# Where the second group's tokens are queued on VectorE in a sorted attention

## The chip, the cores and the metric

The kernel runs on one core of one Trainium2 chip. The metric is the device time of one execution in microseconds; the time of a version is the median over its runs. A profile is one further execution, recorded instruction by instruction. In what follows PE is TensorE (matmuls; PEld its weight loads), DVE is VectorE, ACT is ScalarE, POOL is GpSimd, SP is SyncE. L1454 means line 1454 of the kernel before the change.

## What is computed

Two layers, each an attention-like block and a feed-forward block, on x of 16 x 256 tokens with 512 features, all in float32. Cut to what matters here:

```python
x = x + conv_attention(layernorm(x), k, skip, ctx, ctx)     # layer 0
x = x + routed_ffn(layernorm(x), ...)                       # 8 experts, top 2, and a shared one
x = x + latent_attention(layernorm(x), ctx, seg_id, ...)    # layer 1: the stage that is changed
x = x + ffn(layernorm(x), proj1, proj2, ...)

# latent_attention: 16 heads; a query with segment id s sees the keys s-8 .. s only
q_c = q @ W_dq
scores = (q_nope . k_nope + rope(q_c @ W_qr) . rope(k_rope)) / sqrt(192)
attn = softmax(where((k <= s) & (k >= s - 8), scores, -1e30))
out = (attn @ v) @ W_o
```

The input of the latent attention is the output of the routed layer: per token, its row of x plus two expert rows, each times a gate, then a layernorm.

## The kernel before

The 4096 tokens are sorted by batch and segment id, so that 32 neighbours share a window of 32 keys. The stage `attention_sorted` goes through them in 32 tiles of 128 tokens, T = 0 to 31. Four tiles are a group g with t = T % 4. The queries are made per group: group 0 partly ahead of the loop and partly in its first two passes, group g + 1 while group g is attended. This case is about group 1, tiles 4 to 7, prepared in the passes T = 0 to 3.

What one pass does, in the order in which the program traces it:

- `scores(T)`: small matmuls of queries and window keys into a PSUM tile of its own tag (L1563, L1569). It needs `qn`, `qr` and the window's `kn` and `krz`.
- `weigh(T)`, on DVE: a 32x32-block transpose into `e` (L1579), the mask (L1581), the row maximum (L1585), its subtraction (L1586).
- `values(T-1)`: matmuls of the last pass's attention weights and the gathered keys (L1609), copied out by ACT (L1615).
- `weights(e)`: exp on ACT (L1590), then on DVE the row sums (L1592), reciprocals (L1594), the product (L1595) and a transpose back into `at` (L1597).
- `window(T+1)`: the next window's keys are transposed on PE (L1535, L1540) and copied by ACT (L1537, L1542); its mask is made on DVE (L1548 to L1551).
- `heads`: in T = 0 and 1 the second half of group 0's queries, in every t = 3 the next group's. PE L1501 to L1512; ACT copies (L1517, L1525); the rope on DVE (L1519) and POOL (L1520, L1521). In t = 3, `latents` (L1473, L1484), which `heads` needs, is traced ahead of `values(T-1)`; it reads all four token tiles of the next group.
- `project(T-2)`: 16 matmuls (L1625, 32 in the records), an add on DVE (L1630), a store from POOL's queue (L1631).

`tokens(st, t)` prepares one tile of the next group: two fused multiply-adds of gathered expert rows onto the token row (DVE, L1454, twice), a layernorm by `bn_stats` and `bn_aggr` (DVE, L66 and L68), the inverse root on POOL (L70, L71), the scaling (DVE, L72); then the rope rows' transpose `prr` (PE, L1462) and the row's own transpose `pt` (PE, L99), copied by ACT (L1463, L100).

Rows come by indirect DMAs that POOL issues (all at L1919): `xt` (token rows), `rr` (rope rows), `gw` (the window's keys, four per pass, by `fetch_keys(T + 2)`) and the expert rows, shown as `w<-ygd,slot_s`. The expert rows have four buffers in rotation, two to a tile, so a tile's gathers must wait until the tile two before it has been added. Group 1's tiles are traced at these places: tile 4 at T = 2 after `weigh`; tile 5 at the end of T = 2; tiles 6 and 7 at T = 3 after `weigh` and ahead of `latents`. The gathers of tile 4 are traced at T = 0 and those of tile 5 at T = 1, behind the heads of that pass.

No order is written out for this stage. A program that runs when the kernel is built decides the order of the instructions on each engine: it walks through them with a model of the engines, and gives each engine what is ready, earlier traced work first. `with tc.issue_after(ins):` restricts it: what the block traces on the engine of `ins` is queued behind `ins`. This sets an order only; nothing waits for `ins` to end beyond what an engine does in working through its queue. Instructions in the block on other engines are not held by it.

A tile from a pool takes one of the buffers of its tag. `prr`, `pt`, `pq`, `pqr`, `pqn`, `pkw`, `prw`, `pu` and `po` all have the tag "m" with seven PSUM buffers.

Of the kernel before, what the change touches and what calls it, by code (L numbers as in the profile page):

```python
# [13 lines left out]
ALU = mybir.AluOpType  # L14
# [4 lines left out]
P = 128  # L19
# [15 lines left out]
CQ, WIN = 8, 32  # L35
# [7 lines left out]
class Kernel:  # L43
# [1343 lines left out]
    def attention_sorted(self, fetched, ygd, x3s, end_of_queries):  # L1387
        nc, tc = self.nc, self.tc
        wdq, m0, m1, wqr0, wqr1, nw = self.wdq, self.m0, self.m1, self.wqr0, self.wqr1, self.nw
        fetch, fetch_keys, xs, rrs, gws, _ = fetched  # L1390
        T4 = 4
# [4 lines left out]
        with ExitStack() as ctx:  # L1396
# [41 lines left out]
            def fetch_routed(st, t):  # L1438
                T = st["g"] * T4 + t
                st["y"].append([])  # L1440
                for k in range(2):
                    yt = g_yt[rows_fetched[0] % 4]
                    rows_fetched[0] += 1
                    self.fetch_rows(yt, ygd, self.slot_s[:, k, T : T + 1], NT * P)
                    st["y"][t].append(yt)

            def tokens(st, t):

                T = st["g"] * T4 + t
                if t == 0:  # L1450
                    st["xT"], st["rope"] = g_xT, g_rope
                xt, yts, rr = xs[T], st["y"][t], rrs.pop(T)
                for k in range(2):
                    nc.vector.scalar_tensor_tensor(  # L1454
                        xt, yts[k], self.routes[:, T, 2 + k : 3 + k], xt, ALU.mult, ALU.add
                    )
                xh = tp.tile([P, D], F32, tag="xh", name="xh")
                self.layernorm(xh, xt, small)
                toks = slice(t * P, (t + 1) * P)
                pt = ps_m.tile([P, 2, P], F32, tag="m", name="prr")  # L1460
                for i in range(2):
                    nc.tensor.transpose(pt[:, i, :], rr[:, i, :], self.ident)  # L1462
                nc.scalar.copy(st["rope"][:, :, toks], pt)  # L1463
                self.transposed(st["xT"][:, :, toks], xh, ps_m, "m")
# [60 lines left out]
                        nc.scalar.copy(qn[:, cs, c0 : c0 + CQ], by_chunk(pqn[k][i]))  # L1525
                return turned

            wins, last_at = {}, [None]

            def window(T):  # L1530
                gw = gws.pop(T)
# [21 lines left out]
            def scores(st, T):  # L1553

                w, t = wins[T], T % T4
                s = ps_s.tile([P, 4 * P], F32, tag="s", name="ps")
                for a in range(4):
                    for piece in range(3):
                        for j in range(4):
                            c = t * 16 + a * 4 + j  # L1560
                            r = slice(j * WIN, (j + 1) * WIN)
                            if piece == 0:
                                nc.tensor.matmul(  # L1563
                                    s[r, a * P : (a + 1) * P], w["kn"][:, a, r], qn[:, c, :],
                                    start=(a == 0), stop=False, skip_group_check=True,
                                )
                            else:
                                c0 = a * P + (piece - 1) * (P // 2)
                                nc.tensor.matmul(  # L1569
                                    s[r, c0 : c0 + P // 2], krz[piece - 1][:, a, r], qr[:, c, :],  # L1570
                                    start=False, stop=True, skip_group_check=True,
                                )
                return s

            def weigh(T, s):

                e = ap_.tile([P, 16, WIN], F32, tag="e", name="e")
                flat = e.rearrange("p x k -> p (x k)")
                nc.vector.transpose(flat, s)  # L1579
                e4 = e.rearrange("p (a h) k -> p a h k", h=4)  # L1580
                nc.vector.tensor_tensor(  # L1581
                    e4, e4, wins[T]["mask"].unsqueeze(2).to_broadcast([P, 4, 4, WIN]), ALU.add
                )
                mx = small.tile([P, 16], F32, tag="mx", name="mx")
                nc.vector.tensor_reduce(mx, e, AX.X, ALU.max)  # L1585
                nc.vector.tensor_tensor(e, e, mx.unsqueeze(2).to_broadcast([P, 16, WIN]), ALU.subtract)  # L1586
                return e

            def weights(e):
# [31 lines left out]
            def project(st, T, ut):  # L1621
                po = ps_m.tile([P, D], F32, tag="m", name="po")
                for n in range(HEADS):
                    i, hp = n // HP, n % HP
                    nc.tensor.matmul(  # L1625
                        po, ut[:, n].rearrange("p a j q -> p (a j q)"), nw[:, 2 * hp + i, :],
                        start=(n == 0), stop=(n == HEADS - 1),
                    )
                xt = xs.pop(T)
                nc.vector.tensor_tensor(xt, xt, po, ALU.add)  # L1630
                nc.gpsimd.dma_start(x3s[T // T4][T % T4 * P : (T % T4 + 1) * P, :], xt)  # L1631
# [6 lines left out]
            TH = T4 // 2  # L1638
# [15 lines left out]
            for T in range(NT_ + 2):  # L1654
                g, t = T // T4, T % T4
                if T < NT_:
                    if 3 <= T + 2 < NT_:
                        fetch_keys(T + 2)
                    s = scores(state[g], T)
                    e = weigh(T, s)  # L1660
                    nxt = state.setdefault(g + 1, new(g + 1)) if g + 1 < NG else None

                    if nxt is not None:
                        for k in () if g == 0 else ((0,), (2,), (), ())[t]:
                            fetch((g + 1) * T4 + k)
                            fetch_routed(nxt, k)
                    if nxt is not None and g == 0 and t == 2:
                        with tc.issue_after(turned):
                            tokens(nxt, 0)
                        fetch(T4 + 2)  # L1670
                        fetch_routed(nxt, 2)
                    if nxt is not None and g == 0 and t == 3:
                        for k in range(TH, T4):
                            tokens(nxt, k)
                    if nxt is not None and t == 3:
                        latents(nxt)
                if 1 <= T <= NT_:
                    uts[T - 1] = values(T - 1, ats.pop(T - 1))
                if T < NT_:
                    ats[T] = weights(e)  # L1680
                    if T + 1 < NT_:
                        window(T + 1)
                    if T < 2:
                        for two in range(T * HP // 4, (T + 1) * HP // 4):
                            turned = heads(state[0], two, parts[1])

                        with tc.issue_after(turned):
                            fetch(T4 + T)
                            fetch_routed(nxt, T)
                    if nxt is not None and t == 3:  # L1690
                        for two in range(HP // 2):
                            heads(nxt, two)
                if T >= 2:
                    project(state[(T - 2) // T4], T - 2, uts.pop(T - 2))
                if T >= NT_:

                    if T == NT_:
                        end_of_queries()
                    which = T - NT_
                    xT = self.e_w2[:, which * DC * N : (which + 1) * DC * N].rearrange("p (c x) -> p c x", c=DC)  # L1700
                    for k in range(T4):
                        xt = ap_.tile([P, N], F32, tag="sw", name="xt", bufs=3)
                        nc.sync.dma_start(xt, x3s[which][k * P : (k + 1) * P, :])
                        xh = tp.tile([P, D], F32, tag="xh", name="xh")
                        self.layernorm(xh, xt, small)
                        self.transposed(xT[:, :, k * P : (k + 1) * P], xh, ps_m, "m")
                if T < NT_ and nxt is not None:
                    if g == 0:
                        if t == 2:
                            tokens(nxt, 1)  # L1710
                            fetch(T4 + 3)
                            fetch_routed(nxt, 3)
                    else:
                        if t == 0:
                            fetch((g + 1) * T4 + 1)
                            fetch_routed(nxt, 1)
                        for k in ((0,), (1,), (2, 3), ())[t]:
                            tokens(nxt, k)
                        if t == 1:
                            fetch((g + 1) * T4 + 3)  # L1720
                            fetch_routed(nxt, 3)
# [365 lines left out]
```

## Time and profile before

| | us |
|---|---|
| median of 3 runs | 3074.01 (3070.93 to 3077.48) |
| the profiled execution | 3075.3 |
| its span, first to last instruction | 3073.5 |
| PE busy in it | 3000.4 |
| DVE busy | 1434.6 |
| POOL busy | 921.1 |
| ACT busy | 661.8 |
| the sorted attention, passes T = 0 to 3, until the scores of T = 4 begin | about 1283 to 1452 |

A row of the timeline gives start and duration in us, engine, line, operation, output and input names, shapes and count; in square brackets the idle time of the engine ahead of it and what ended that. The busy time of PE is pipelined work and no measure of its peak; what counts here is where it is idle, and the granted clock: TensorE runs at full (1.00) or half (0.50) clock in these rows.

### The profile page before, as it was taken

How to read it: one execution, taken by the hardware profiler on the slowest of the kernel's cores; microseconds unless marked ns; L12 is line 12 of the kernel's file. 1: busy time of each engine (PE TensorE's matmuls, PEld its weight loads, DVE VectorE, ACT ScalarE, POOL GpSimd, SP SyncE). 2: the span in 40 equal slices, each digit the busy share in tenths (PEclk: the TensorE clock that was granted, in tenths of full speed). 3: DMA queues.
4: the chain of work that ended last, by engine and by line, in shares of the span. 5: the costliest groups of instructions: out<-in, count | busy, mean ns of one | idle time of the engine just before them, and what ended most of it. 6: DMA issues, size and time to landing. Idle time of an engine off the chain costs nothing.

```text
span 3073.5 us, 34728 instructions
## 1 busy us (share of the span) xinstructions
PE 3000.4 (98%) x12825; PEld 1529.7 (50%) x12825; DVE 1434.6 (47%) x2652; ACT 661.8 (22%) x1250; POOL 921.1 (30%) x1270
## 2 busy tenths in 40 slices
PE   7999999999999999889999999999999999999998
PEld 4444444444455666554554554454444444444443
DVE  6877777776764444443433433443333222222222
ACT  1111111111111111243333323324121111111110
POOL 2233233232223300165545555534110300301201
PEclk9999999999999999989999999999999999999999
DMA  4232221211115653311211221212120100100100
GB/s 118 70 107 88 59 63 57 67 60 60 56 41 184 208 164 129 111 52 45 86 53 53 74 66 46 69 53 70 58 103 28 55 14 14 55 10 11 45 0 29
DMA packets 119218, 209.87 MB, mean 68 GB/s; under 512 B 27592, under 2 KB 47976, under 8 KB 118400
## 3 DMA queue, kind: packets, MB, share of 16 engines
q1 hardware_dynamic: 90752, 125.63, 13.6%
q0 software_dynamic: 28288, 81.92, 8.3%
q8 instruction: 105, 1.72, 0.2%
q14 instruction: 73, 0.60, 0.1%
HBM read 140.12 MB, written 67.37 MB: 68 GB/s over the span
## 4 chain that ended last, share of the span: by engine, by line
PE 87%; DVE 6%; issue 4%; POOL 2%; DMA 1%; ACT 0%; SPq 0%; POOLq 0%; DVEq 0%; ACTq 0%
PE y L292 15%; PE po L1879 14%; PE ph L1821 13%; PE po L1625 11%; PE phg L895 4%; PE pog L914 4%; PE pqn L1504 4%; PE pout L503 3%; PE ph L490 3%; PE pqr L1501 2%; PE pqn L1512 2%; PE pt L99 2%; PE pqr L1508 1%; DVE pr L297 1%; PE ptg L884 1%
## 5 line engine op out<-in xcount | busy, mean ns | idle before, releaser
L292 PE MATMUL y<-kv,ut 128*128 128x512 f32 x1280 | 562.4, 594 | 0.6 <-DVE pr L297 0.6
L1625 PE MATMUL po<-nw,w 128*128 128x512 f32 x1024 | 445.7, 593 | 0.0
L1879 PE MATMUL po<-p,ht 128*128 128x512 f32 x1024 | 445.1, 592 | 0.0
L292 PEld LDWEIGHTS y<-kv,ut 128*128 128x128 f32 x1280 | 242.1, 191 | 295.6 <-issue 286.1
L1625 PEld LDWEIGHTS po<-nw,w 128*128 128x128 f32 x1024 | 192.0, 190 | 235.1 <-issue 229.6
L1879 PEld LDWEIGHTS po<-p,ht 128*128 128x128 f32 x1024 | 192.7, 190 | 233.4 <-issue 232.2
L1821 PE MATMUL ph<-w,w 128*128 128x512 f32 x640 | 281.2, 592 | 0.0
L297 DVE TENSOR_TENSOR pr<-y,cT 128x512 f32<-128x512 f32 x256 | 174.7, 682 | 143.3 <-PE y L292 143.3
L1883 DVE TENSOR_TENSOR res<-res,po 128x512 f32<-128x512 f32 x128 | 87.8, 686 | 315.4 <-PE po L1879 315.4
L1821 PEld LDWEIGHTS ph<-w,w 128*128 128x128 f32 x640 | 121.5, 190 | 152.6 <-issue 152.6
L304 DVE TENSOR_REDUCE oT<-pr 128x64 f32<-128x512 f32 x256 | 175.7, 686 | 8.8
L274 DVE TENSOR_TENSOR kv<-pvt,cT 128x512 f32<-128x512 f32 x256 | 174.1, 681 | 0.0
L1919 POOL DMA_INDIRECT gw<-kvd,keys_of x128 | 133.3, 1041 | 49.9 <-issue 37.8
L267 POOL TENSOR_TENSOR xt<-xt,sk 128x512 f32<-128x512 f32 x32 | 40.7, 1271 | 338.8 <-DVE sk L266 298.4
L1519 DVE TENSOR_TENSOR w<-pqr,w 128x512 f32<-128x512 f32 (+1 forms) x72 | 45.4, 632 | 203.0 <-ACT sw L1517 189.5
L895 PE MATMUL phg<-w,xTg 128*128 x568 | 134.6, 380 | 0.2
L914 PE MATMUL pog<-w,hT 128*128 x284 | 133.6, 593 | 0.0
L1504 PE MATMUL pqn<-w,m 128*128 128x512 f32 (+1 forms) x288 | 117.0, 548 | 7.2 <-ACT kn L1537 7.1
L490 PE MATMUL ph<-xT,w_s 128*128 128x512 f32 x256 | 118.4, 607 | 0.0
L1821 PE MATMUL ph<-xT,w 128*128 128x512 f32 x256 | 116.4, 592 | 0.0
L1835 ACT ACTIVATE ht<-ht,p1b 128x512 f32<-128x512 f32 x96 | 69.3, 722 | 212.7 <-DVE ht L1840 212.7
L503 PE MATMUL pout<-w_s,ht 128*128 128x512 f32 x256 | 113.6, 593 | 0.0
(291 smaller groups left out, 3773.9 us busy)
## 6 DMA issues: line engine op xcount, KB each, us to landing
xg<-xgd SPq DMA_DIRECT2D x71, 256.0 KB, 2.7
ygd<-y SPq DMA_DIRECT2D x71, 256.0 KB, 2.0
xt<-in_x_dram SPq DMA_DIRECT2D x32, 256.0 KB, 3.5
ct<-in_ctx_dram SPq DMA_DIRECT2D x32, 256.0 KB, 3.4
ut<-in_kt_dram SPq DMA_DIRECT2D x32, 256.0 KB, 2.6
w<-in_w_dram SPq DMA_DIRECT2D x8, 1024.0 KB, 5.5
x1d<-xt SPq DMA_DIRECT2D x32, 256.0 KB, 2.9
x3s<-xt POOLq DMA_DIRECT2D x32, 256.0 KB, 2.9
```

The costliest lines, as they stand in the source:

```text
L274: nc.vector.tensor_tensor(c["kv"][half][:, mc, :].rearrange("p (b j i) -> p b j i", i=NH, j=NH), c["vt"][:, mc, cols].rearrange("p (b i) - ...
L292: c["conv"] = nc.tensor.matmul(y, ut[:, (lc - mc) * P : (lc - mc + 1) * P], kv[:, mc, :], start=(mc == 0), stop=(mc == lc),).ins
L297: nc.vector.tensor_tensor(pr, y.rearrange("p (b j i) -> p b j i", i=NH, j=NH), cT[:, lc, cols].rearrange("p (b i) -> p b i", i=NH) .unsque ...
L304: nc.vector.tensor_reduce(c["oT"][:, lc, cols].rearrange("p (b j) -> p b j", j=NH), pr, AX.X, ALU.add)
L490: nc.tensor.matmul(ph, w["sw1"][:, c, f * P : (f + 1) * P], xT[:, c, :], start=(c == 0), stop=(c == DC - 1),)
L503: nc.tensor.matmul(po, st["ht"][f][:, tok], w["sw2"][:, f, :], start=(f == 0), stop=(f == NC_ - 1))
L895: nc.tensor.matmul(ph, xT[:, c, :], w1[:, c, bass.ds(e * EH, EH)], start=(c == 0), stop=(c == DC - 1))
L914: nc.tensor.matmul(po, hT[:, q, :], w2[:, bass.ds(e * (EH * D // P) + q * D, D)], start=(q == 0), stop=(q == EH // P - 1),)
L1504: nc.tensor.matmul(pqn[k][i], m0[:, 2 * hp + i, :], q0, start=True, stop=False)
L1625: nc.tensor.matmul(po, ut[:, n].rearrange("p a j q -> p (a j q)"), nw[:, 2 * hp + i, :], start=(n == 0), stop=(n == HEADS - 1),)
L1821: nc.tensor.matmul(ph, w[:, c, :], x[:, c, :], start=(start and c == 0), stop=(c == half - 1), skip_group_check=True,)
L1879: nc.tensor.matmul(po, ht[f, i // T4][:, toks], w2[:, f, :], start=(f == fs[0]), stop=(f == fs[-1]))
```

## The change

`weigh` keeps its last DVE instruction, the subtraction of the maximum, as `last_e[0]`. The tokens of group 1 are then traced inside `issue_after` blocks: tile 4 behind the subtraction of T = 2 (it keeps its older block, which concerns POOL), tile 5 behind the last transpose of T = 2 (`last_at[0]`, L1597), tiles 6 and 7 behind the subtraction of T = 3. This queues their L1454, L66, L68 and L72 behind those instructions on DVE. Nothing is added to the computation or taken from it, and the places where things are traced stay the same. Groups 2 to 7 are traced by other lines and are not touched.

```diff
-            wins, last_at = {}, [None]
+            wins, last_at, last_e = {}, [None], [None]
...
-                nc.vector.tensor_tensor(e, e, mx.unsqueeze(2).to_broadcast([P, 16, WIN]), ALU.subtract)
+                last_e[0] = nc.vector.tensor_tensor(
+                    e, e, mx.unsqueeze(2).to_broadcast([P, 16, WIN]), ALU.subtract
+                ).ins
                 return e
...
                     if nxt is not None and g == 0 and t == 2:
-                        with tc.issue_after(turned):
+                        with tc.issue_after(turned), tc.issue_after(last_e[0]):
                             tokens(nxt, 0)
                         fetch(T4 + 2)
                         fetch_routed(nxt, 2)
                     if nxt is not None and g == 0 and t == 3:
-                        for k in range(TH, T4):
-                            tokens(nxt, k)
+                        with tc.issue_after(last_e[0]):
+                            for k in range(TH, T4):
+                                tokens(nxt, k)
...
                         if t == 2:
-                            tokens(nxt, 1)
+                            with tc.issue_after(last_at[0]):
+                                tokens(nxt, 1)
                             fetch(T4 + 3)
                             fetch_routed(nxt, 3)
```

## The prediction

> **What bounds the kernel now.** I read the page first. TensorE is busy nearly everywhere, so a change pays or costs only what it does to TensorE's gaps:
>
> ```profile
> PE 3000.4 (98%) x12825; PEld 1529.7 (50%) x12825; DVE 1434.6 (47%) x2652; ACT 661.8 (22%) x1250; POOL 921.1 (30%) x1270
> ```
>
> The changed lines trace work of steps T = 2 and 3 of the sorted attention. I looked for those by stretches of time (length, busy time of PE, PEld, DVE, ACT and POOL, then the granted clock, DMA share, GB/s):
>
> ```profile
> 1333.00:1349.00 16.00, 15.99 (x215) 12.71 (x206) 8.39 (x17) 11.06 (x25) 8.27 (x11) 1.00 0.04 11
> 1349.00:1380.00 31.00, 17.95 (x183) 13.49 (x182) 14.92 (x31) 10.19 (x26) 24.41 (x27) 0.72 0.38 105
> 1380.00:1452.00 72.00, 71.22 (x330) 32.34 (x328) 21.70 (x44) 28.86 (x54) 40.93 (x42) 1.00 0.17 49
> ```
>
> One stretch is bad: 31 us with 13.05 us of idle TensorE and a mean clock of 0.72; it is the step from T = 1 to T = 2. Behind it TensorE is full. The timeline says why:
>
> ```profile
> 1345.00 0.72 DVE L1579 STREAM_TRANSPOSE e<-ps 128x512 f32<-128x512 f32 x1 [0.75 <-PE ps L1569]
> 1351.20 0.75 DVE L1454 SCALAR_TENSOR_TENSOR xt<-w,routes,xt 128x512 f32<-128x512 f32 x1 [5.48 <-DMA w<-ygd,slot_s]
> 1351.87 0.69 DVE L1581 TENSOR_TENSOR e<-e,mask 128x512 f32<-128x512 f32 x1
> ...
> 1354.50 0.68 DVE L1586 TENSOR_TENSOR e<-e,mx 128x512 f32<-128x512 f32 x1
> 1355.74 0.57 ACT L1537 COPY kn<-pkw 128x512 f32<-128x512 f32 x1
> 1356.36 1.22 PE L1504 MATMUL pqn<-w,m 128*128 128x256 f32 x2 [7.14 <-ACT kn L1537]
> ```
>
> The softmax of T = 1 is cut after its first instruction by the tokens of the second group, though they are traced at T = 2: VectorE sits 5.48 us before L1454 until gathered rows land, L1581 queues behind that, then exp and the kn copy on ScalarE, and TensorE loses 7.14 us. Call the second group's tiles k0 to k3. The gather at 1352.22 waits for an L1454, so it fetches into k0's buffers: it is k2's, and k2 too is joined in this softmax (1355.76, 1357.32). k1 and k3 follow at 1375.31 and 1381.64.
>
> **Part 1, the stall that goes: a gain.** Every VectorE instruction of k0 and k2 that stands between L1579 and L1597 of T = 1 (four L1454, one L66, one L68) leaves it. An uncut softmax runs from the start of L1579 to the end of L1586 in 2.97 us (T = 4: 1454.27 to 1457.24), so T = 1's ends at 1347.97. ScalarE is at its pu copies until 1348.11, exp takes 0.63, kn is copied by 1349.2, where TensorE stops today. The 7.14 us go, and so does the half clock after them: TensorE worked 5.9 us (1356.36 to 1362.3) at 0.5, half of it lost, 3.0. heads of T = 1 end near 1356 instead of 1365.7.
>
> What is late next is POOL, in order. Today 1349.99 to 1363.22 goes to k2's two gathers, the four of the key window, and two of the third group; then the rope adds (L1520, L1521) take 5.74 until 1368.96, and scores of T = 2 waits for them. k2's gathers (they overwrite k0's buffers) and the third group's (k2's buffers) now have to follow the moved L1454, so they leave. The key gathers stay: 1350.29 + 5.55 + 5.74 = 1361.6. The rope part of scores takes 3.16 after a gap, as today, and ends at 1364.8 against 1372.2: 7.4 us earlier.
>
> **Part 2, k0 behind the softmax of T = 2: most of that given back.** What may TensorE do while k0 is prepared? Here I chose a reading that decides everything. The program traces k0's transposes (pt, L99) ahead of values(1), window(3) and project(0), and all write the PSUM tag "m". Could they overtake? The start of the stage answers:
>
> ```profile
> 1297.19 1.11 PE L99 MATMUL pt<-ident,xh 128*128 128x128 f32 x4 [8.26 <-DVE xh L72]
> ...
> 1300.40 1.06 PE L1535 MATMUL pkw<-ident,gw 128*128 128x128 f32 x4
> ```
>
> TensorE stood 8.26 us for an L72 although the window behind it had its keys (gathers issued 1058.03 to 1072.34, 4.7 us to landing). From there to 1564 I found only scores (its own PSUM tag) moved against traced order. L66 of k2 also waited until right after that of k1 (1377.83, 1379.11), 20 us after its data. So I take one tag's tiles to be given out in traced order: no overtaking.
>
> Then TensorE is idle from the end of scores(2), 1364.8, to pt of k0. L1586 ends 3.0 later (1367.8), two L1454, L66 and L68 with gaps follow (2.3: 1370.1), then L70 and L71 on POOL (0.9), L72 to pt (0.74): 1371.8 if POOL is free, 1372.4 with a softmax instruction slipped in. POOL is not: k1's gathers (today 1369.11 to 1372.75, 3.64) and three rr gathers (4.1) run from 1361.6 to 1369.4, and k2's two gathers become ready with L1454, before L68. That gathers go first, the present trace shows (L68 had ended at 1379.19):
>
> ```profile
> 1377.60 1.19 POOL L1919 DMA_INDIRECT w<-ygd,slot_s  x1 [0.30 <-DVE xt L1454]
> 1379.09 1.00 POOL L1919 DMA_INDIRECT w<-ygd,slot_s  x1 [0.30 <-issue]
> 1380.11 0.29 POOL L70 TENSOR_TENSOR ln_rs<-ln_mv,eps 128x1 f32<-128x1 f32 x1
> ```
>
> Two more are 2.64: L70 at 1372.3, L72 at 1373.15, pt at 1373.9. Today:
>
> ```profile
> 1375.53 0.70 PE L99 MATMUL pt<-ident,xh 128*128 128x128 f32 x4 [3.36 <-DVE xh L72]
> 1379.67 13.90 PE L1625 MATMUL po<-nw,w 128*128 128x512 f32 x32
> 1395.73 0.41 PE L1569 MATMUL ps<-w,krz 128*32 128x64 f32 x16
> 1398.38 1.94 PE L1473 MATMUL pq<-w,w_dq 128*64 128x512 f32 x8 [0.78 <-ACT w L100]
> ```
>
> From pt on, both kernels come out of a gap at half clock, so the rest is equal. Gain: **1.6** (3.1 with L70 ahead of the gathers).
>
> k1, queued behind the last transpose of T = 2, costs nothing: it is ready about 1386, covered by the 13.7 us of project(0), and TensorE wants it near 1391. Without that cover it would cost some 9, as k0 does (1364.8 to 1373.9).
>
> **Part 3, k2 and k3 behind the softmax of T = 3: a new stall.** Today both are ready early, and latents starts 2.25 after the end S of scores(3) (1396.13 to 1398.38). latents needs all four tiles, is traced next, and holds up values(2), window(4), heads and project(1) by the same tag. From S: L1586 ends at 3.0. Four L1454 at 0.67, two L66 at 0.6, two L68 and a softmax instruction take 4.2: S + 7.2. On POOL four gathers of the third group are released by those L1454 and, as above, go first: the queue has the store and xt until S + 2.8 as today (1398.94) and one rr gather, so four at 1.32 from S + 4.1 end at S + 9.4. Two L70 and two L71 with gaps, 1.6: S + 11.0. L72 to the end of ScalarE's copy of pt is 2.1 (1374.79 to 1376.87): with L72 of k3 at S + 11.2, latents starts at S + 13.3. Against 2.25 that is **11.0** lost. Bounds: POOL free gives S + 10.1 (7.9 lost); S + 14.6 (12.4) if both further rr gathers, which end today at S + 5.4 (1401.55), go first too.
>
> To this comes the clock. The Trainium skill ("TensorE: Matmul & The Clock Gate", Part 1) says that one idle window of about 3.4 us halves the clock, and about 3.4 us of sustained work brings it back: 1.7 lost. The row above lost 3.0 after 7.14 idle. With the row, 3.0; with the rule, 1.3 less in the total. I take the row. The rule also speaks against the change: it makes two gaps longer than that where there was one.
>
> **Sum.** -1.6 + 11.0 + 3.0 = +12.4 on the profiled execution, 3075.3 + 12.4 = 3087.7. The median, 3074.0, is 1.3 below it: **3086**. The other ends together, -3.1 + 7.9 + 1.7 = 6.5, give 3080.5; the upper ones (12.4; 3.4, which is two such windows at half clock; no gain at T = 2) 3090. From T = 4 on TensorE is full (112.00 of 112.00 us from 1452), so the shift stays to the end.
>
> **Rivals.** First, **faster**: the order is free, and window, values and project fill the waits. Then project(0) starts at 1364.8 + 3.6 = 1368.4 instead of 1379.84, 11.4 earlier; project(1), 13.7, covers T = 3, some 1 us is lost in it: 3064. It decides once project may pass an unready pt. For it: scores was pulled ahead of an unready latents at 1327. Against it: the 8.26 us above. Second, **no change that can be told**: the waits are there but cancel. With rope ahead of the key gathers on POOL, scores(2) starts 3.0 after its last inputs, near 1359, unchilled, and pt of k0 comes at 1368.5, 7.0 gained; with POOL free at T = 3, 7.9 + 1.7 lost: +2.6, 3077. Against it: the key gathers are traced before heads and ran first. That the change does nothing is excluded: the old order breaks its edges.
>
> **Chances.** Forecast case 0.66 (own range 3079 to 3092), cancelling 0.20, free order 0.14. A measurement here tells about 0.2%, 6.1 us, from no change. The forecast's lower tail and the upper one of the cancelling case about balance: slower 0.66, same 0.20, faster 0.14. The range 3074 to 3093 leaves out the free order and the tails.
>
> **What would show it.** Right: no L1454 between L1579 and L1586 of T = 1; the 7.1 us wait at L1504 gone; two waits of pt for L72, some 8 to 9 us after scores(2) and 10 in all after scores(3); latents about 13 us after scores(3), at half clock; POOL gathering ahead of L70. Wrong: project matmuls ahead of pt or latents, or a latents start within 5 us of scores(3).

## The result, and the profile after

The changed kernel takes 3088.97 us (median of 6 runs, 3084.05 to 3090.74) against 3072.98 us for the kernel before, measured beside it (6 runs): a ratio of 1.0048, 95% interval 1.0035 to 1.0061. The profiled execution took 3090.74 us with a span of 3089.0 us, 15.5 us more than before. Below L1586 the lines of the changed kernel stand two further down (the last transpose is L1599, values L1611, project L1627), and the gathers are L1923.

First the page of the changed kernel, its row of busy times by engine:

```profile
PE 3004.8 (97%) x12825; PEld 1530.0 (50%) x12825; DVE 1435.0 (46%) x2652; ACT 661.9 (21%) x1250; POOL 923.8 (30%) x1270
```

The instruction counts are those of before and the busy times hardly differ. PE has 4.4 us more for the same work, so most of the 15.5 us, 11.1, must be idle TensorE. The waits of TensorE between 1283 and 1480 us (what waited and for whom; sum in us, times, longest) show where. After:

```profile
PE pt L99 <- DVE xh L72: 18.2, 3, 9.2
PE pt L99 <- DVE ln_mv L68: 11.0, 1, 11.0
PE ps L1563 <- ACT w L1525: 2.5, 1, 2.5
```

Before:

```profile
PE pt L99 <- DVE xh L72: 12.4, 3, 8.3
PE pqn L1504 <- ACT kn L1537: 7.1, 1, 7.1
```

The 7.1 us at L1504 are gone. In their place stand a pt wait of 9.2 us at T = 2, which was 3.4, and one of 11.0 us at T = 3, which was not there. (The 8.3 us wait is at the stage's start, in both.)

An offset has to be taken out before times are compared: the after execution reaches the stage 2.66 us late (the pt behind that 8.3 us wait starts at 1299.85 instead of 1297.19), from work the change does not touch; a second profile of the same kernel reaches it at 1297.43. In the timeline of T = 1 the softmax is no longer cut:

```profile
1347.57 0.72 DVE L1579 STREAM_TRANSPOSE e<-ps 128x512 f32<-128x512 f32 x1 [0.76 <-PE ps L1569]
...
1350.12 0.68 DVE L1586 TENSOR_TENSOR e<-e,mx 128x512 f32<-128x512 f32 x1
...
1351.99 0.70 PE L1504 MATMUL pqn<-w,m 128*128 128x256 f32 x2 [0.20 <-ACT kn L1537]
```

At T = 2 the scores end early, and then nothing runs on TensorE until pt, while on POOL two gathers stand ahead of L70:

```profile
1366.80 0.65 PE L1569 MATMUL ps<-w,krz 128*32 128x64 f32 x16
...
1372.37 0.99 POOL L1923 DMA_INDIRECT w<-ygd,slot_s  x1 [0.30 <-DVE xt L1454]
...
1373.67 1.38 POOL L1923 DMA_INDIRECT w<-ygd,slot_s  x1 [0.31 <-DVE mask L1551]
1375.07 0.20 POOL L70 TENSOR_TENSOR ln_rs<-ln_mv,eps 128x1 f32<-128x1 f32 x1
...
1376.65 1.09 PE L99 MATMUL pt<-ident,xh 128*128 128x128 f32 x4 [9.20 <-DVE xh L72]
```

At T = 3, from the end of the scores at S = 1398.15, the timeline shows who is late:

```profile
1397.74 0.41 PE L1569 MATMUL ps<-w,krz 128*32 128x64 f32 x16
...
1401.09 2.73 DVE L1454 SCALAR_TENSOR_TENSOR xt<-w,routes,xt 128x512 f32<-128x512 f32 x4
...
1403.02 1.02 POOL L1923 DMA_INDIRECT w<-ygd,slot_s  x1 [0.31 <-issue]
...
1404.35 1.01 POOL L1923 DMA_INDIRECT w<-ygd,slot_s  x1 [0.30 <-issue]
1404.94 0.17 DVE L68 BATCH_NORM_AGGREGATE ln_mv<-ln_st 128x2 f32<-128x6 f32 x1
...
1406.96 1.00 POOL L1923 DMA_INDIRECT w<-ygd,slot_s  x1 [0.30 <-issue]
1407.98 0.21 POOL L70 TENSOR_TENSOR ln_rs<-ln_mv,eps 128x1 f32<-128x1 f32 x1
1408.27 0.56 POOL L71 TENSOR_TENSOR ln_rs<-ln_rs,mhalf 128x1 f32<-128x1 f32 x1
1408.87 0.55 DVE L72 TENSOR_SCALAR xh<-xt,ln_mv,ln_rs 128x512 f32<-128x512 f32 x1 [3.20 <-POOL ln_rs L71]
1409.33 0.17 DVE L68 BATCH_NORM_AGGREGATE ln_mv<-ln_st 128x2 f32<-128x6 f32 x1
...
1409.56 1.09 PE L99 MATMUL pt<-ident,xh 128*128 128x128 f32 x4 [11.05 <-DVE ln_mv L68]
...
1410.49 0.55 DVE L72 TENSOR_SCALAR xh<-xt,ln_mv,ln_rs 128x512 f32<-128x512 f32 x1 [0.71 <-POOL ln_rs L71]
...
1412.31 0.59 ACT L100 COPY w<-pt 128x512 f32<-128x512 f32 x1 [0.77 <-PE pt L99]
...
1412.95 3.46 PE L1473 MATMUL pq<-w,w_dq 128*64 128x512 f32 x8 [0.68 <-ACT w L100]
```

The four L1454 run right behind the softmax, but L70, a 0.21 us addition, comes 2.9 us after the end of the L68 it needs: POOL is in the middle of four gathers at 1.3 us each. They fetch expert rows for the third group into the buffers that the L1454 themselves freed. The waits view files the 11.05 us under L68, but pt reads the output of L72 (`xh`): the releaser is the L72 that ended at 1409.42, and behind it POOL. L68 of the second tile stands behind L72 of the first on DVE, so the second tile starts its way through POOL only at 1409.33. latents (L1473) begins 14.8 us after S instead of 2.25, and at half clock (3.46 us for what took 1.94). The granted clock is the third number from the right:

```profile
1409.50:1413.00 3.50, 2.65 (x12) 1.91 (x12) 2.79 (x9) 1.45 (x3) 2.01 (x3) 0.50 0.11 42
1413.00:1416.30 3.30, 3.30 (x8) 0.71 (x8) 1.77 (x5) 0.00 (x0) 2.67 (x3) 0.54 0.36 98
1416.30:1420.00 3.70, 3.70 (x14) 1.47 (x12) 1.23 (x2) 1.16 (x2) 0.59 (x2) 1.00 0.32 94
```

### The profile page after: what moved, and what is told of

It is laid out like the page before. It is cut to its first block, busy times and chain, and to the rows that moved or that the text cites. A ratio compares the mean times of both kernels' runs of the same rounds, so it can differ in the third digit from the quotient of the medians.

```text
span 3089.0 us, 34732 instructions
## 1 busy us (share of the span) xinstructions
PE 3004.8 (97%) x12825; PEld 1530.0 (50%) x12825; DVE 1435.0 (46%) x2652; ACT 661.9 (21%) x1250; POOL 923.8 (30%) x1270
## 4 chain that ended last, share of the span: by engine, by line
PE 86%; DVE 6%; issue 4%; POOL 2%; DMA 1%; ACT 0%; SPq 0%; POOLq 0%; DVEq 0%; ACTq 0%
PE y L292 15%; PE po L1883 14%; PE ph L1825 12%; PE po L1627 10%; PE phg L895 4%; PE pog L914 4%; PE pout L503 4%; PE pqn L1504 3%; PE ph L490 3%; PE pqr L1501 2%; PE pqn L1512 2%; PE pt L99 2%; PE pqr L1508 1%; DVE pr L297 1%; DVE kv L274 1%
## 5 line engine op out<-in xcount | busy, mean ns | idle before, releaser
L1627 PE MATMUL po<-nw,w 128*128 128x512 f32 x1024 | 445.9, 593 | 0.0
L1627 PEld LDWEIGHTS po<-nw,w 128*128 128x128 f32 x1024 | 192.3, 190 | 235.2 <-issue 229.7
L1923 POOL DMA_INDIRECT gw<-kvd,keys_of x128 | 132.4, 1034 | 54.3 <-issue 37.5
L1519 DVE TENSOR_TENSOR w<-pqr,w 128x512 f32<-128x512 f32 (+1 forms) x72 | 45.5, 632 | 207.7 <-ACT sw L1517 195.0
L1504 PE MATMUL pqn<-w,m 128*128 128x512 f32 (+1 forms) x288 | 116.6, 547 | 0.2 <-ACT kn L1537 0.2
```

Of the source, the lines that this page charges most:

```text
L1504: nc.tensor.matmul(pqn[k][i], m0[:, 2 * hp + i, :], q0, start=True, stop=False)
L1627: nc.tensor.matmul(po, ut[:, n].rearrange("p a j q -> p (a j q)"), nw[:, 2 * hp + i, :], start=(n == 0), stop=(n == HEADS - 1),)
```

## The experiments

One yardstick is used throughout: in a profile, the start of project(2) counted from the pt at the stage's start, 159.0 us before (1456.2 less 1297.19) and 172.4 us after. It says what the stage lost without the offset. The runs were made on three chips; every ratio is against the kernel before on the same chip (medians 3075.41, 3105.45 and 3074.20 us). Each yardstick comes from one profile.

### One half of the change at a time (first chip)

Without the edge at T = 3:

```diff
-                        with tc.issue_after(last_e[0]):
-                            for k in range(TH, T4):
-                                tokens(nxt, k)
+                        for k in range(TH, T4):
+                            tokens(nxt, k)
```

> The two edges of T = 2 alone (tiles 4 and 5); tiles 6 and 7 traced at T = 3 without an edge. Theory (TensorE's queue holds everything behind the tokens' transposes, so each edge costs the chain behind its softmax): T = 2 as in the changed kernel, its wait of about 9 us for pt of tile 4 and project(0) only some 1 us earlier than before; latents within 3 us of the end of scores(3). Time 3072, from 3068 to 3076, no change against before. Rival (the wait at T = 2 is what makes the changed kernel slower, T = 3 only follows): 3080 or more, with latents still late.

Measured: 3074.48 us, ratio 0.9998 (0.9990 to 1.0007), yardstick 158.4. The pt wait at T = 2 is 9.2 us as in the changed kernel; there is none at T = 3.

Without the edges at T = 2:

```diff
-                        with tc.issue_after(turned), tc.issue_after(last_e[0]):
+                        with tc.issue_after(turned):
...
-                            with tc.issue_after(last_at[0]):
-                                tokens(nxt, 1)
+                            tokens(nxt, 1)
```

> The edge of T = 3 alone (tiles 6 and 7); tiles 4 and 5 as before. Theory: the stall of T = 1 stays, 7 us at L1504, since tile 4 is still joined there; pt of tile 4 comes some 3 us earlier, because tile 6's gathers no longer delay POOL; latents about 14 us after the end of scores(3), 14 us lost with the half clock. Time 3083, from 3080 to 3087. Rival (tiles 6 and 7 are only late because tiles 4 and 5 were moved): latents within 5 us of scores(3), time about 3070.

Measured: 3086.78 us, ratio 1.0037 (1.0023 to 1.0051), yardstick 174.0 in an execution that was 5.7 us above its own median. Its waits keep the old stall and have the new one:

```profile
PE pt L99 <- DVE xh L72: 12.4, 3, 8.2
PE pt L99 <- DVE ln_mv L68: 11.1, 1, 11.1
PE pqn L1504 <- ACT kn L1537: 7.1, 1, 7.1
```

One part of this expectation failed: counted from the pt at the stage's start, pt of tile 4 comes 0.5 us earlier than before, not 3.

The loss lies in T = 3: its edge alone has it all, within the noise. At T = 2 a wait of 7.1 us is removed, and what is won by it, 0.9 us by the medians and 0.6 by the yardstick, can't be told from nothing: pt of tile 4 waits instead.

### Does traced order hold TensorE back?

The prediction rested on one PSUM tag's tiles being handed out in traced order. Two edits ask that. The first gives `prr` and `pt` a tag of their own (one buffer, six left for "m"):

```diff
-            ps_m = pool("s_ps_m", 7, space=PSUM)
+            ps_m = pool("s_ps_m", 6, space=PSUM)
+            ps_t = pool("s_ps_t", 1, space=PSUM)
...
-                pt = ps_m.tile([P, 2, P], F32, tag="m", name="prr")
+                pt = ps_t.tile([P, 2, P], F32, tag="t", name="prr")
...
-                self.transposed(st["xT"][:, :, toks], xh, ps_m, "m")
+                self.transposed(st["xT"][:, :, toks], xh, ps_t, "t")
```

> The changed kernel with the tokens' transposes (prr, pt) in a PSUM tag of their own, one buffer, and six buffers instead of seven for all else; nothing is traced elsewhere. Theory (one tag's tiles are given out in traced order): values(1), window(3) and project(0) go ahead of pt of tile 4, the 9 us wait of T = 2 goes and project(0) starts some 11 us earlier than in the changed kernel; the wait of T = 3 stays, because latents has the tag of values and project and is traced ahead of them. Time 3075 plus what six buffers cost, from 3070 to 3082. Rival (the order of tracing itself holds TensorE, not the tag): the order of TensorE stays as it was and the time at 3089.

Measured: 3124.4 us, ratio 1.0161 (1.0147 to 1.0175): the time missed the expectation by far. The order did not, but the wait that was to go with it stayed. TensorE's timeline at T = 2 (lines stand one or two further down here; L1570 is the end of the scores, L1612 values(1), L1536 window(3), L1628 project(0)):

```profile
1369.93 0.67 PE L1570 MATMUL ps<-w,krz 128*32 128x64 f32 x16
...
1370.53 2.08 PE L1612 MATMUL pu<-at,gw 32*128 32x128 f32 x28
1372.54 0.96 PE L1536 MATMUL pkw<-ident,gw 128*128 128x128 f32 x4
1373.34 0.60 PE L1541 MATMUL prw<-ident,gw 128*128 128x128 f32 x4
1373.78 3.60 PE L1628 MATMUL po<-nw,w 128*128 128x512 f32 x8
1385.61 1.12 PE L99 MATMUL pt<-ident,xh 128*128 128x128 f32 x4 [8.23 <-DVE xh L72]
```

values, window and a quarter of project(0) now pass the unready pt, which they do in neither profile of the changed kernel, nor in that of before. So it is the tag that held them. pt still waits 8.2 us: TensorE's order is fixed when the kernel is built, and the builder put pt after 8 of 32 matmuls, far earlier than L72 came. Behind the window, the next key gathers were free sooner too and went ahead on POOL (1376.76 to 1381.67, with L70 at 1382.99), so pt came 15 us after the scores instead of 9.2.

The kernel before with the same tags is the control (second chip):

> The kernel before with the tokens' transposes in a PSUM tag of their own and six buffers for the rest: the control of the version of the changed kernel with that. Theory (the tag split costs by itself, six buffers are too few for heads): slower than before by 20 us or more, about 3105, and the version of the changed kernel above it by 15 to 20. Rival (the split is free and only the change makes its version slow): 3073.

Measured: 3145.67 us, ratio 1.0125 (1.0109 to 1.0140). Most of the 1.0161 is thus the price of the split, six buffers in "m" for one. What the change costs on top would be 1.0161/1.0125 = 1.0036, but the two were measured on different chips, and for a difference this small that is only a hint.

The second edit keeps the tag and moves the place where things are traced: tile 4 behind project(0), and tiles 6 and 7, `latents` and `heads` behind project(1), with the change's edges kept.

```diff
                 if T >= 2:
                     project(state[(T - 2) // T4], T - 2, uts.pop(T - 2))
...
+                            with tc.issue_after(turned), tc.issue_after(last_e[0]):
+                                tokens(nxt, 0)
...
+                        if t == 3:
+                            with tc.issue_after(last_e[0]):
+                                for k in range(TH, T4):
+                                    tokens(nxt, k)
+                            latents(nxt)
+                            for two in range(HP // 2):
+                                heads(nxt, two)
```

> All edges kept, but the tracing moved: tile 4 behind project(0) in T = 2, and tiles 6 and 7, latents and heads behind project(1) in T = 3. DVE still does the tokens behind the softmax; TensorE has values, window and project to do meanwhile. Theory: no wait of pt for L72 over 1 us, the stall of T = 1 gone; scores(2) still waits for the rope on POOL, some 4 us. project(0) about 13 us earlier than before: 3060, from 3056 to 3064. Rival (the chain over DVE and POOL is itself too slow, wherever TensorE's part is traced): 3080 or more, with latents waiting 10 us behind project(1).

Measured: 3075.12 us, ratio 1.0001 (0.9993 to 1.0010), yardstick 160.2: a miss. The traced-order half of it held: project(0) starts at 1367.8 instead of 1379.7 and no pt waits over 0.41 us at T = 2 and 3. That gain was gone by project(2). In the timeline of this kernel the third group's tokens, freed early, got onto DVE ahead of the heads:

```profile
1414.98 1.54 DVE L1454 SCALAR_TENSOR_TENSOR xt<-w,routes,xt 128x512 f32<-128x512 f32 x2 [6.77 <-DMA xt<-x1d,order]
...
1421.03 1.27 DVE L1519 TENSOR_TENSOR w<-pqr,w 128x512 f32<-128x512 f32 x2
...
1421.76 1.09 PE L1501 MATMUL pqr<-w,w_qr 128*128 128x512 f32 x1 [2.54 <-DVE w L1519]
...
1451.93 0.43 PE L1569 MATMUL ps<-w,krz 128*32 128x64 f32 x16 [1.58 <-POOL w L1521]
```

DVE stands 6.77 us before a row that has not landed, and the rope (L1519) queues behind it: the fault that the change set out from, one group later. The heads also lost the 13.9 us of project(1) that had covered ACT and POOL, so the scores of T = 4 wait for the rope. From project(0) to project(2) TensorE is idle for 7.5 us here and for 0.8 before; the stretch is 12.7 us longer, and what is more than the idle time was not traced to its end.

### Who is late: POOL's gathers

In the changed kernel the gathers for tile 6 and for three of the four tiles of every later group are queued on POOL behind the last L71 (`self.normed`):

```diff
-                            fetch((g + 1) * T4 + k)
-                            fetch_routed(nxt, k)
+                            with tc.issue_after(self.normed):
+                                fetch((g + 1) * T4 + k)
+                                fetch_routed(nxt, k)
```

and so at two other places where such rows are fetched ahead (one of them is tile 6's).

> The changed kernel with the gathers of tile 6 queued on POOL behind tile 4's L71, and those of the third group behind the last L71 traced, so that the layernorms of tiles 4, 6 and 7 go ahead of the gathers. Theory (POOL's gathers are a part of both waits): pt of tile 4 waits 7 us instead of 9.2 after scores(2); latents starts about 11 us after scores(3) instead of 14.8. Time 3083, from 3080 to 3087. Rival (the waits are DVE's work alone): waits unchanged, 3089.

Measured on the second chip: 3105.84 us, ratio 1.0007 (0.9999 to 1.0016). That is more than the theory gives. Either the gathers cost 12 us, or that chip shows less of the change. The same kernel was run once more on a third chip, beside the changed kernel itself.

> The changed kernel once more, beside the kernels below on one chip. If the change's cost does not depend on the chip, the ratio to the kernel before is 1.0048 as in the first measurement (1.0035 to 1.0061). If the second chip simply shows less of it, as the ratio 1.0007 of the run with later POOL gathers would then have to be read, it is 1.002 or less here too.

> The changed kernel with tile 6's and the third group's row gathers queued on POOL behind the layernorms, measured again beside the changed kernel itself. Theory: of the changed kernel's loss of about 15 us, POOL's gathers ahead of the layernorm's last instruction take about 4 us (2.8 at T=3, 1.1 at T=2); the ratio to before is then about 1.0035, 1.3 per mille below the changed kernel's. Rival: they take about 12 us, the ratio stays at 1.0007 while the changed kernel's is 1.0048.

> Only tile 6's gathers (issued at T=2 and used at T=3, in the first attention stage) are moved behind the layernorm; those of the third and later groups stay. If the gain of the wider edit lies in this stage, this kernel gives nearly all of it (same ratio within 0.05 per cent as the wider edit). If it comes from the later groups, this kernel is within 0.05 per cent of the changed kernel less the 1.1 us of T=2.

| | median, us | ratio to before | yardstick, us | pt wait, T = 2 and 3 |
|---|---|---|---|---|
| before | 3074.20 | | 159.0 | 3.4, none |
| changed kernel | 3087.88 | 1.0044 (1.0030 to 1.0058) | 172.3 | 9.2, 10.5 |
| all gathers behind | 3084.65 | 1.0035 (1.0022 to 1.0049) | 168.7 | 8.2, 8.2 |
| only tile 6's behind | 3086.33 | 1.0037 (1.0023 to 1.0051) | 172.2 | 8.2, 11.1 |

(The yardstick and the waits of before are those of its profile.) The wider edit is worth 3.2 us by the medians and 3.6 by the yardstick, near the 4 expected; the 12 us of the second chip do not come again. Tile 6's gathers account for 1.0 us of the wait at T = 2 and for nothing at T = 3 (nor does the yardstick show that 1.0), so what blocks L70 at T = 3 are the third group's. The ratios of the last three kernels overlap, and it is the traces, not the ratios, that tell them apart. The timeline of the wider edit at T = 3 (the scores end at 1390.84; L70 now follows L68 at once):

```profile
1397.64 0.17 DVE L68 BATCH_NORM_AGGREGATE ln_mv<-ln_st 128x2 f32<-128x6 f32 x1
1397.89 0.18 POOL L70 TENSOR_TENSOR ln_rs<-ln_mv,eps 128x1 f32<-128x1 f32 x1 [7.98 <-DVE ln_mv L68]
...
1399.45 1.09 PE L99 MATMUL pt<-ident,xh 128*128 128x128 f32 x4 [8.24 <-DVE ln_mv L68]
...
1402.83 3.68 PE L1473 MATMUL pq<-w,w_dq 128*64 128x512 f32 x8 [0.67 <-ACT w L100]
```

With POOL out of the way 8.24 us are still waited: softmax, four L1454, two L66 and the layernorm in a row on DVE, with no matmul allowed beside them. latents starts 12.0 us after the scores, in place of 14.8. POOL is the smaller part of the loss, the place of the tokens the larger.

Why the second chip gave 1.0007 for this kernel is open, and the changed kernel was not measured there. Its pt waits are the same on both chips (8.1 and 8.2 us on the second), so the stall is not what differs. The traces do differ behind the stage, where the edit moves gathers too. From project(2) to the last group's latents, the second chip has 616.1 us for this kernel and 621.4 for each of the two kernels of the next section that ran there; the third chip has 616.4 for it and 614.5 to 614.7 for the three others. The edit may thus save some 5 us in the later groups on the second chip and nothing on the third. This compares different kernels, one profile each, and shows no cause.

### A version that keeps the gain

If T = 3's edge is the loss and traced order the limit at T = 2, the edges of T = 2 should pay once tile 4 is traced behind project(0), with no edge at T = 3:

```diff
-                    if nxt is not None and g == 0 and t == 2:
-                        with tc.issue_after(turned), tc.issue_after(last_e[0]):
-                            tokens(nxt, 0)
-                        fetch(T4 + 2)
-                        fetch_routed(nxt, 2)
...
-                        with tc.issue_after(last_e[0]):
-                            for k in range(TH, T4):
-                                tokens(nxt, k)
+                        for k in range(TH, T4):
+                            tokens(nxt, k)
...
                         if t == 2:
+                            with tc.issue_after(turned), tc.issue_after(last_e[0]):
+                                tokens(nxt, 0)
+                            fetch(T4 + 2)
+                            fetch_routed(nxt, 2)
```

> The edges of T = 2 kept, that of T = 3 taken away, and tile 4 traced behind project(0). Theory: TensorE has project(0) to do while DVE and POOL prepare tile 4, so project(0) starts some 12 us earlier than before, as it did with everything traced late; latents and heads stay ahead of project(1), so what that version gave back (the copies and the rope behind heads uncovered, the third group's tokens among them) stays covered; tiles 6 and 7 may come 2 to 4 us late. Time 3064, from 3060 to 3069. Rival (the tokens' chain over DVE and POOL takes as long as before, and the time won at T = 2 only comes back as a wait at latents): 3073, with latents waiting 8 us or more.

Measured on the second chip: 3097.03 us, ratio 0.9976 (0.9966 to 0.9985): 8.4 us below the kernel before on that chip, where 10 were expected. With tile 4's gathers put behind the heads of T = 1 as well:

> As the one with tile 4 behind project(0), and tile 4's gathers (three, 3.9 us of POOL) moved behind the heads of T = 1 too, with tile 5's. Theory: the rope of T = 1 no longer waits for them on POOL, scores(2) ends some 3 us earlier; but the four tiles' gathers all follow the rope, so tiles 6 and 7 come up to 4 us later. Time 3064, from 3060 to 3069, about equal to the version without this. Rival (POOL is no limit here): no difference in either place.

Measured: 3100.61 us, ratio 0.9984 (0.9975 to 0.9992), not better: its median is 3.6 us higher on the same chip. With tile 6's gathers behind the layernorm instead (third chip):

> Tile 4's tokens traced behind project(0), with the waits of T=2 kept and none at T=3, and tile 6's gathers behind the layernorm on POOL. Against the same kernel without the last edit (ratio 0.9976): if POOL's gathers delay nothing any more once the tokens stand behind project(0), the ratio stays 0.9976; if the remaining waits of 1.4 and 1.2 us come from them, it falls to about 0.9970.

Measured: 3069.93 us, ratio 0.9984 (0.9977 to 0.9990), yardstick 153.8, so 5.2 us won in the stage. The waits did not shrink as the second branch of the expectation had it (the one for L68 is 3.4 us, not 1.4); whether this last edit helps can't be told, since the two kernels ran on different chips. The two stretches that had 13.05 and 0.78 us of idle TensorE before are in this kernel (busy time of TensorE first, granted clock third from the right):

```profile
1349.00:1380.00 31.00, 27.49 (x216) 17.63 (x215) 16.14 (x34) 13.72 (x32) 24.84 (x27) 0.89 0.31 90
1380.00:1452.00 72.00, 66.74 (x418) 32.38 (x420) 22.19 (x42) 27.11 (x51) 43.50 (x44) 0.98 0.19 57
```

The rows that decide are the early project(0) and the late pt of tile 6:

```profile
1370.10 13.90 PE L1627 MATMUL po<-nw,w 128*128 128x512 f32 x32
...
1388.30 0.63 PE L99 MATMUL pt<-ident,xh 128*128 128x128 f32 x4 [3.43 <-DVE ln_mv L68]
```

The first stretch has 3.51 us of idle TensorE in place of 13.05, the second 5.26 in place of 0.78: 9.5 us won and 4.5 given back, in the wait for tile 6's layernorm (3.4) above all. This execution reaches the stage 2.8 us late; stretches moved by as much have the same idle times. Without that offset project(0) starts 12.3 us earlier than before, project(2) 5.2.

## Why the prediction was right, and where it was not

**Part 1.** Right: no L1454 inside the softmax of T = 1, the wait at L1504 down from 7.14 to 0.20. The scores of T = 2 end at 1367.45, or 1364.8 without the offset, and 1364.8 was predicted, through the key gathers and the rope on POOL, whose last addition ends at 1361.5 without the offset (1361.6 predicted).

**Part 2.** Right in mechanism. pt comes at 1376.65, 1374.0 without the offset, against 1373.9. Gathers stand ahead of L70 at 1372.37 and 1373.67. Of the 1.5 us won at pt, 0.9 is left at the start of project(0) (1381.45 less 2.66 = 1378.8, against 1379.7); "the rest is equal" was 0.7 too kind, and the half clock behind this gap lasts longer than behind the old one: granted 0.50 and 0.72 in the first two stretches of 3.4 us from pt, where before had 0.57 and 0.93. By the end of scores(3) 0.65 is left (1398.15 less 2.66 = 1395.49, against 1396.14), so this gain of 1.6 was mis-sized by 1.0. The reading of the tag, on which all hung, was shown by the tag split. That k1 costs nothing was right.

**Part 3.** Right in mechanism, mis-sized in two terms that cancel, which is luck. latents starts at S + 14.8 and not at S + 13.3, so 12.5 us are lost and not 11.0. The gathers of experts' rows end at S + 9.8 (9.4 predicted). The next 0.7 us is the step "Two L70 and two L71 with gaps", which took the two tiles as one batch: on DVE, L68 of the second tile is queued behind L72 of the first, so its L72 starts at S + 12.3 and not S + 11.2. The last 0.3 us lies between that L72 and the end of the copy, 2.4 where 2.1 was taken. The clock, taken at 3.0 from the row of before, is less where I put it: 1.5 at L1473, the cold transposes ahead of it being already inside the 12.5. From S to values(2) it took 21.8 us (1419.97 less 1398.15) against 7.74, 14.1 lost where 11.0 + 3.0 = 14.0 were predicted. Row and rule can be compared here: the half clock lasts from 1409.5 to about 1416, 6.5 us, in which the transposes (1.09 for 0.60 twice, 0.63 for 0.44) and L1473 lost 2.7 (granted 0.50, then 0.54, then 1.00). The estimate of 1.7 from the one window of sustained work that the Trainium skill names ("TensorE: Matmul & The Clock Gate", Part 1) was too little here, where TensorE worked for only 2.65 us of the first 3.5; the row was near.

**Sum.** +12.4 predicted for the profiled execution, +13.4 by the yardstick in both profiles of the changed kernel. It is the 14.1 lost in Part 3 less the 0.65 won in Part 2. The span of the first, +15.5, has the offset on top; the second, with an offset of 0.24, has +12.8.

**Rivals.** The free order is excluded: nothing with tag "m" passed an unready pt while the tag was one. In the version that lets it happen by its place in the trace, project(0) is as early as that rival had it (1367.3 without the offset, 1368.4 there), and 7.1 of the 12.3 us are given back by project(2). (The prediction's start of project(0) today, 1379.84, is 0.17 late: the row starts at 1379.67.) The cancelling case fell because the key gathers ran ahead of the rope again, and POOL was not free at T = 3.

## What to carry to other kernels

An instruction moved behind another on one engine takes with it all that other engines' fixed orders put behind it: here TensorE stood through a whole softmax and layernorm because the transposes were traced, in the same PSUM tag, ahead of 14 us of ready work. Move the traced place together with the edge, so that TensorE has ready work ahead of the wait. Moving every place did not pay here (1.0001); moving tile 4 alone, with no edge at T = 3, did. And look at the in-order queue of the engine that does the tiny steps: four gathers of 1.3 us each stood ahead of a 0.2 us addition, and putting the gathers behind it was worth 3.6 us of the 13.4 lost.

## What the hardware showed that was not expected

- A gather costs POOL's queue 1.3 us (1.00 us and 0.30 between two), and instructions of 0.2 us wait for whole rows of them: L70 came 2.9 us after its input.
- The clock fell to half without one long idle time. In the last version the scores of T = 2 run at half clock (granted 0.50 from 1362 to 1364, 0.66 us for 8 matmuls instead of 0.42), where the longest single wait in the 3 us before was 1.10 us. TensorE was busy for 1.98 of the 3.5 us before them (0.94 granted in the last 1.5):

```profile
1361.18 0.48 PE L1611 MATMUL pu<-at,gw 32*128 32x128 f32 x2 [1.10 <-ACT w L1525]
1362.01 0.66 PE L1563 MATMUL ps<-w,kn 128*32 128x128 f32 x8 [0.35 <-ACT w L1525]
```

- The same kernel differs from chip to chip by 1% (before: 3074.2, 3075.4 and 3105.5 us), and the ratio of an edit can differ with it: the changed kernel with later gathers had 1.0007 on the slower chip and 1.0035 on another, with intervals that do not overlap. Here ratios from different chips could not be put side by side to a tenth of a per cent.
